# Linear layer's four outer products in one joint tree, and another order of the first loads, in a fused factorization kernel

## The chip, the cores and the metric

The kernel runs on one core of a Trainium2 chip. The time is the device time of one execution in microseconds (us); of several runs the median is given. A profile is one further execution, recorded by the hardware profiler. The engines are TensorE (PE: matmuls, with PEld for its weight loads), VectorE (DVE), ScalarE (ACT), GpSimd (POOL) and SyncE (SP, which here only issues DMAs). Each works through its own list of instructions in order and waits on semaphores for the others.

## The reference

```python
def _L0_rec_ref(x, weight, lin_w, lin_b):   # x 1024x512, weight 64x512x512, lin_w 512x512
    out_lin = x @ lin_w.T + lin_b
    xv = jnp.einsum('bf,efm->bem', x, weight)
    zp = jnp.einsum('bf,efm->bem', jnp.square(x), jnp.square(weight))
    interaction = 0.5 * jnp.sum(jnp.square(xv) - zp, axis=1)
    return out_lin + interaction
```

All is float32. The bulk of the work is `xv`, 64 products of 1024x512 by 512x512. `zp` is summed over the 64 embeddings, so it is one product of squared x with the sum of the squared weights.

## The kernel before

**Products of seven.** Every product of 2x2 blocks is done with seven block products in place of eight (Winograd's form), on two levels. The outer level splits x into A11, A12, A21, A22 (halves of the batch and of the features) and the weight into w11, w12, w21, w22. Outer product i (1 to 7) has its own left operand X_i, a sum of blocks of A, and its own right operand: w11, w21, w22, w21 after an accumulate, T1, T2 or w12 after an accumulate, for i = 1, 2, 3, 4, 5, 6, 7. Here T1 = w11 + w12 and T2 = w11 + w12 + w22. Inside outer product i, `tree` (from line 650) again makes seven block products P1 to P7, each of two 128x512 matmuls. Their right operands are the four blocks of the outer operand and four sums of them, t1 to t4, which GpSimd makes (VectorE makes t1 and t2 of the very first tree). Their left operands are seven slots of the tile `x_all`, four raw blocks and three sums s1, s2, s4, made once at the start by VectorE (`x_sum`, line 413). For the outer operands X5, X7, X6, X3 the four blocks are themselves sums of A's blocks; they are called R5, R7, R6, R3.

**Loops.** The weight comes in 16 groups (`group`, from line 908). A group loads its four quadrants (`load`), forms T1 and T2 (`outer_sum`, line 612), and runs seven trees in the order 1, 6, 2, 7, 5, 4, 3 (1, 2, 6, 7, 5, 4, 3 in the first group). The results are squared by ScalarE, reduced over the embeddings by VectorE (line 339) and collected.

**Inside a tree** the seven products go to PSUM banks in a fixed way: P5 and then P3 to b3, P1 and P2 to b1, P6, P7 and P4 to one of two banks b2. ScalarE copies P5 to a p5 tile, P3 to a p53 tile and P1 into b2, where P6 is added by TensorE. Then results are taken out of the bank after P6 (tile 1), after P2 (tile 0), after P7 (tile 3) and after P4 (tile 2). Since P7 and P4 accumulate in the bank that P6 used, each waits for the add that took the result before. In the first tree these results are the tiles oa0 to oa3: VectorE adds P6's bank to p53 into oa1 and P7's bank to p5 into oa3, both line 316.

**T1 and T2.** In groups 1 to 15 both are made by DMAs: a plain load of w11 and accumulating loads issued by GpSimd (`load_more`, line 604). In group 0 VectorE adds them from the loaded quadrants, T1 in two halves, then T2 in two halves.

**The linear layer** uses the same blocks. Its outer products 1, 2, 4 and 5 are done directly (`lin_product`, line 449) ahead of the first tree; P1 and P2 go in pieces as x and lin_w land. Outer products 6, 7 and 3 are done in one `joint_tree` (line 814), a tree whose seven products run for all members in one go, with 256-column matmuls (line 826). `lin_inner` (line 490) lets GpSimd make the sums of the members' right operands; `lin_tree` (from line 884) adds the members' results up and sends them out by accumulating DMAs. The joint tree is interleaved with the second and third tree of group 0.

**What sets the order.** All operations go through a planner (`Plan`). TensorE's order is fixed by keys: tree number times 7 plus a place from the table `PLACE` (`PLACE_0` in the first tree). The planner lists the other engines' operations by the latest time at which they are due, with costs and landing times written down in the kernel, and emits one list for each engine. The first loads are issued outside it (lines 354 to 386): x and lin_w in pieces on the queues of SP and ACT, each with a written-down landing time.

**Tiles.** x's blocks land in oa0 to oa3 and lin_w's in ob0 and ob1; both sets serve later as results of the trees. `c` (three), `p5` (three), `p53` (three) and `wsq` (two) are rings of tiles.

The lines touched are the tables at the top, the tiles, the first loads, `lin_inner`, `outer_sum`, `tree`, `lin_tree` and `group`.

Of the kernel before, what the change touches and what calls it, by code (L numbers as in the profile page):

```python
# [16 lines left out]
P = 128  # L17
# [8 lines left out]
PLACE = {5: -6, 3: -2, 1: 0, 6: 3, 2: 4, 7: 6, 4: 9}  # L26
PLACE_0 = {**PLACE, 5: -6, 1: -3, 3: -2, 6: -1}
PE, DVE, ACT, POOL, SP = "PE", "DVE", "ACT", "POOL", "SP"
# [3 lines left out]
class Plan:  # L32
# [44 lines left out]
    def order(self):  # L77
# [27 lines left out]
        times = [self.HOP]  # L105
        done, late, nxt, wire = [], 0.0, 0, 9.0

# [95 lines left out]
def kernel(  # L203
# [81 lines left out]
    for q in ("w11", "w12", "w21", "w22a", "w22b", "T1", "T2"):  # L285
        make(q, [P, 2, 2, N])
    for pos in range(4):
        make(f"oa{pos}", half)
        make(f"ob{pos}", half)
    t_ring = {k: ring(f"t{k}", 2, [P, N]) for k in range(1, 5)}  # L290
    p5_ring, p53_ring = ring("p5", 3, half), ring("p53", 3, half)
    c_ring, wsq_ring = ring("c", 3, half), ring("wsq", 2, half)
    make("b1", [P, G, N], ps)
# [61 lines left out]
    def load_x(h, k, lo, hi, at):  # L355

        n, r = f"oa{2 * h + k // KH}", k % KH
        nc.sync.dma_start(buf[n][:, r, lo * Q:hi * Q], x_src[:, k, h * H + lo * Q:h * H + hi * Q])
        for u in range(lo, hi):
            landing((n, r, u), at)  # L360

    def load_lw(queue, ks, c, at):

        l, r = f"ob{ks[0] // KH}", ks[0] % KH
        queue.dma_start(
            buf[l][:, r:r + len(ks), ts(c, N // 2)],
            lw_src[:, ks[0]:ks[0] + len(ks), ts(c, N // 2)],
        )
        for k in ks:
            landing((l, k % KH, c), at)  # L370
# [10 lines left out]
    load_lw(nc.sync, [2, 3], 1, 9.2)  # L381
    for at, k in enumerate((2, 3, 0, 1)):
        load_x(1, k, 0, 2, 10.0 + 0.8 * at)
    nc.scalar.dma_start(bias[:], lin_b)
    landing("bias", 9.5)
# [13 lines left out]

    a_buf = {"A11": "oa0", "A12": "oa1", "A21": "oa2", "A22": "oa3"}  # L400

# [73 lines left out]

    lw_quad = [buf[f"ob{q}"][:, :, ts(c, HM)] for q in range(2) for c in range(2)]
    lw_names = [tuple((f"ob{q}", r, c) for r in range(KH)) for q in range(2) for c in range(2)]
    lt = {
# [11 lines left out]
    def lin_inner():  # L490


        t23 = buf["w22b"].rearrange("p c k n -> p (c k n)")[:, N:3 * N].rearrange(
            "p (i k m) -> p i k m", i=2, k=KH
        )
        flat = buf["ob0"].rearrange("p a (k m) -> p a k m", m=P)
        for (ap, own), t, outs in (
            ((t23, lt_names[2] + lt_names[3]), {k: flat[:, :, k - 1] for k in range(1, 5)}, (6, 7)),
            (rhs[3], {
                k: buf["ob1"][:, (k - 1) // 2, ts((k - 1) % 2, P)] for k in range(1, 5)  # L500
            }, (3,)),
        ):
            b11, b21, b12, b22 = (
                ap[:, k, ts(c, P)] if len(outs) == 1 else ap[:, :, k, ts(c, P)]
                for c in range(2) for k in range(KH)
            )
            names = {k: (("li", outs[0], k),) for k in range(1, 5)}
            more = own + ("quads", "R6")
            for k, x, y, r in (
                (1, b12, b11, more),  # L510
                (2, b22, t[1], more + names[1]),
                (3, b22, b12, more),
                (4, b21, t[2], more + names[2]),
            ):
                costs, emit = two_input(POOL, t[k], x, y, True, len(outs) * P)
                plan.add(costs, emit, r, names[k])
            for at, i in enumerate(outs):
                def of(z):
                    return z[:, at] if len(outs) > 1 else z

                tt[i] = {
                    1: (of(b11), own), 2: (of(b21), own), 3: (of(b22), own),
                    **{p: (of(t[k]), names[k]) for p, k in ((4, 4), (5, 1), (6, 2), (7, 3))},
                }

# [13 lines left out]
    def lin_copy(n, bank, c, sign):  # L539

        for u in range(2):
            plan.add(
                {ACT: 0.56},
                lambda _, u=u: nc.scalar.activation(
                    buf[n][:, u, :], buf[bank][:, u, :], AF.Identity,
                    bias=bias[:, 2 * c + u:2 * c + u + 1], scale=sign,
                ),
                ((bank, u), "bias"), ((n, u),),
            )
        used(n, (n, 0), (n, 1))  # L550
# [6 lines left out]
    def used(*names):  # L557

        plan.add({NONE: 0.0}, None, (), names)

    lin_product(1, "b2_1", True, -1000, by_k=True)
    lin_copy("ob3", "b2_1", 0, 1.0)
    act(buf["ob2"], buf["b2_1"], None, ("b2_1",), ("ob2",))
    lin_product(2, "b1", True, -999, by_k=True)
    lin_last("ob3", "b1", 1)
    lin_store("ob3", 0, 0)
    lin_product(4, "b2_0", True, -998)
    lin_copy("c_2", "b2_0", 0, 1.0)
    lin_store("c_2", 1, 0)
    lin_product(5, "b1", True, -997)  # L570
    flat = buf["w22b"].rearrange("p c k n -> p (c k) n")
    buf["outer7"], buf["negative"] = flat[:, 0::3], flat[:, 1:3]
    used("outer7", ("lt", 1), ("lt", 4))
    lin_copy("outer7", "b1", 1, -1.0)
    lin_store("outer7", 1, 1)
    lin_store("outer7", 0, 1)
    used("quads", *(("ob0", r, c) for r in range(KH) for c in range(2)), ("ob1", 0, 0), ("ob1", 1, 0))
    lin_inner()
# [11 lines left out]

    for n in a_buf.values():
        used(n, *((n, r, u) for r in range(KH) for u in range(2)))


# [5 lines left out]
    def load(g, q):  # L600
        n = w(g, QUAD[q])
        dma(buf[n], weight[g, q], (), (n,), 3.5)

# [8 lines left out]
    def outer_sum(g, which):  # L612
        if g == 0 and which < 3:
            o, a, b = (("T1", "w11", "w12"), ("T2", "w22a", "T1"))[which - 1]
            for c in range(NCB):
                costs, emit = two_input(DVE, buf[o][:, c], buf[a][:, c], buf[b][:, c], False)
                plan.add(costs, emit, (a, b), (o,), both=True)
        elif which < 3:
            n = f"T{which}"
            dma(buf[n], weight[g, 0], (), (n,), 3.5)  # L620
            for q in (1, 3)[:which]:
                load_more(n, weight[g, q])
        elif which == 3:
            load_more("w12", weight[g, 3])
        else:
            load_more("w21", buf["T2"], ("T2",))
# [23 lines left out]
    def tree(s, g, i, order):  # L650
# [3 lines left out]
        for k, a, b, reads in (  # L654
# [6 lines left out]
            costs, emit = two_input(engine, buf[t[k]], a, b, True, 512)  # L661
            plan.add(costs, emit, reads, (t[k],), both=engine == DVE)
        rhs = {
            1: (b11, r), 2: (b21, r), 3: (b22, r), 4: (buf[t[4]], t[4]),
            5: (buf[t[1]], t[1]), 6: (buf[t[2]], t[2]), 7: (buf[t[3]], t[3]),
# [148 lines left out]
    def joint_tree(at, members):  # L814
# [67 lines left out]
        to(2, b2)  # L882

    def lin_tree():

        results = {6: "ob3", 7: "outer7", 3: c_ring()}
        for n in results.values():
            used(n, *((n, pos) for pos in range(4)))
        joint_tree(2, [(i, i, n) for i, n in results.items()])
        for n in results.values():  # L890
            used(n, *((n, pos) for pos in range(4)))
        used("negative", ("lt", 2), ("lt", 3))
        names = tuple(("li", i, k) for i in (6, 3) for k in range(1, 5))
        used("ob0", "quads", *names)
        used("ob1", *lw_names[3], *names)
        o6, o7, o3 = results.values()
        for to, o, a, b, kind in (
            (None, "ob2", "ob2", o6, "a + b"),
            ((0, 1), o3, "ob2", o3, "-a - b"), ((1, 0), o7, "ob2", o7, "a + b"),
        ):  # L900
            x_sum((o,), buf[o], buf[a], buf[b], kind, (a, b), 1024)
            if to:
                lin_add(o, *to)
        act(buf["negative"], buf[o7], "negative", (o7,), ("negative",))
        lin_add("negative", 1, 1)
        used("w22b", "outer7", "negative")

    def group(g, before={}):
        acc_name[g] = acc_ring()
        for q in range(4):  # L910
            load(g, q)
        outer_sum(g, 1)
        outer_sum(g, 2)
        w_squares(g, "w12")
# [31 lines left out]

    def parts(n):
        return tuple((n, pos) for pos in range(4))

    def part(n, pos):  # L950
        q, c = divmod(pos, 2)
        return buf[n][:, c, ts(q, Q)]

    def in_parts(n, *more):
        used(n, *parts(n), *more)

    def halves_of(n):
        for u in range(2):
            buf[n, u] = buf[n][:, u]
            in_parts((n, u), n)  # L960

# [270 lines left out]
```

## Time and profile before

| what | value |
|---|---|
| median of 3 runs | 1402.33 us (1402.14 to 1402.83) |
| the profiled execution | 1403.01 us |
| its span, first to last instruction | 1401.2 us |
| TensorE busy | 1395.3 us |
| VectorE, GpSimd, ScalarE busy | 1099.9, 1053.3, 714.9 us |
| first tree's first matmul | 19.26 us after the start |
| last matmul's start | 1396.93 us |

The span leaves out 1.8 us of the profiled execution's time. In the rows of the profile a matmul in float32 appears as two records, and the next one's start, not its modelled end, tells how long TensorE was held. L316 is the helper's line for every sum of two tiles on VectorE or GpSimd, so a row is told by its tiles: `t<-w` is a sum for a tree, `x_all<-x_all` a sum of x's blocks, `oa<-b,p` a result taken out of a PSUM bank.

### The profile page before, as it was taken

How to read it: one execution, taken by the hardware profiler on the slowest of the kernel's cores; microseconds unless marked ns; L12 is line 12 of the kernel's file. 1: busy time of each engine (PE TensorE's matmuls, PEld its weight loads, DVE VectorE, ACT ScalarE, POOL GpSimd, SP SyncE). 2: the span in 40 equal slices, each digit the busy share in tenths (PEclk: the TensorE clock that was granted, in tenths of full speed). 3: DMA queues.
4: the chain of work that ended last, by engine and by line, in shares of the span. 5: the costliest groups of instructions: out<-in, count | busy, mean ns of one | idle time of the engine just before them, and what ended most of it. 6: DMA issues, size and time to landing. Idle time of an engine off the chain costs nothing.

```text
span 1401.2 us, 10709 instructions
## 1 busy us (share of the span) xinstructions
PE 1395.3 (100%) x3314; PEld 629.8 (45%) x3314; DVE 1099.9 (78%) x987; ACT 714.9 (51%) x756; POOL 1053.3 (75%) x750
## 2 busy tenths in 40 slices
PE   9999999999999999999999999999999999999998
PEld 4544444444444444444444444444444444444454
DVE  7998696877959788696877959678696877959676
ACT  4555473545736456373544636355373544636444
POOL 4796776958778586786958678686786958678994
PEclk9999999999999999999999999999999999999999
DMA  7495574827749285582817538183572817538363
GB/s 270 94 221 162 138 180 121 226 74 180 205 121 232 90 196 164 135 221 82 225 51 180 153 99 206 49 196 120 132 178 84 222 53 180 154 97 207 101 165 113
DMA packets 55815, 212.90 MB, mean 152 GB/s; under 512 B 21520, under 2 KB 23056, under 8 KB 33872
## 3 DMA queue, kind: packets, MB, share of 16 engines
q0 software_dynamic: 13136, 84.81, 31.5%
q1 hardware_dynamic: 40352, 125.12, 25.6%
q10 hardware_dynamic: 2272, 2.30, 0.5%
q8 instruction: 27, 0.44, 0.1%
q14 instruction: 28, 0.23, 0.0%
HBM read 180.75 MB, written 14.02 MB: 139 GB/s over the span
## 4 chain that ended last, share of the span: by engine, by line
PE 96%; DVE 1%; DMA 1%; ACT 0%; issue 0%; SPq 0%; DVEq 0%
PE b L673 93%; PE b L826 2%; PE b L465 1%; DMA c<-xT 1%; PE b L1145 1%; DMA oa<-xT 0%; DVE p L316 0%; DVE c L316 0%; DVE ob L316 0%; DVE w_sum L339 0%; ACT ob L332 0%; DVE oa L316 0%; DVE acc L339 0%; ACT c L332 0%; ACT b L328 0%
## 5 line engine op out<-in xcount | busy, mean ns | idle before, releaser
L673 PE MATMUL b<-t,x_all 128*128 128x512 f32 x1792 | 806.4, 592 | 0.2 <-DVE oa L316 0.2
L673 PEld LDWEIGHTS b<-t,x_all 128*128 128x128 f32 x1792 | 340.2, 190 | 426.1 <-issue 417.3
L673 PE MATMUL b<-w,x_all 128*128 128x512 f32 x768 | 358.1, 592 | 0.0
L316 POOL TENSOR_TENSOR t<-w 128x512 f32<-128x512 f32 x127 | 171.3, 1349 | 148.5 <-PE b L673 78.1
L328 ACT COPY p<-b 128x1024 f32<-128x1024 f32 x165 | 165.6, 1003 | 171.0 <-PE b L673 166.2
L673 PEld LDWEIGHTS b<-w,x_all 128*128 128x128 f32 x768 | 145.9, 190 | 183.7 <-issue 182.5
L316 POOL TENSOR_TENSOR t<-w,t 128x512 f32<-128x512 f32 x127 | 171.8, 1353 | 55.1 <-PE b L673 54.8
L332 ACT ACTIVATE oa<-oa 128x1024 f32<-128x1024 f32 x124 | 129.5, 1057 | 144.2 <-DVE oa L316 144.2
L328 ACT COPY b<-b 128x1024 f32<-128x1024 f32 (+1 forms) x114 | 113.5, 996 | 135.7 <-PE b L673 132.0
L673 PE MATMUL b<-T,x_all 128*128 128x512 f32 x384 | 180.3, 592 | 0.0
L339 DVE TENSOR_REDUCE acc<-oa 128x16 f32<-128x1024 f32 x124 | 148.8, 1211 | 36.7 <-ACT oa L332 36.7
L339 DVE TENSOR_REDUCE w_sum<-wsq 128x16 f32<-128x1024 f32 x128 | 153.6, 1209 | 0.3 <-ACT wsq L332 0.2
L332 ACT ACTIVATE c<-c 128x1024 f32<-128x1024 f32 x77 | 79.6, 1055 | 131.6 <-DVE c L316 88.2
L316 DVE TENSOR_TENSOR oa<-b,p 128x1024 f32<-128x1024 f32 x95 | 115.7, 1218 | 33.7 <-PE b L673 33.5
L316 POOL TENSOR_TENSOR t<-T 128x512 f32<-128x512 f32 x64 | 85.7, 1339 | 53.2 <-issue 31.3
L673 PEld LDWEIGHTS b<-T,x_all 128*128 128x128 f32 x384 | 73.0, 190 | 91.0 <-issue 89.4
L316 DVE TENSOR_TENSOR p<-b,p 128x1024 f32<-128x1024 f32 x79 | 96.4, 1220 | 20.9 <-PE b L673 16.8
L316 DVE TENSOR_TENSOR ob<-b,p 128x1024 f32<-128x1024 f32 x48 | 58.6, 1221 | 64.7 <-PE b L673 64.4
L332 ACT ACTIVATE wsq<-w 128x1024 f32<-128x1024 f32 x96 | 98.3, 1054 | 12.0 <-DMA w<-weight 11.1
L316 POOL TENSOR_TENSOR t<-T,t 128x512 f32<-128x512 f32 x64 | 82.4, 1288 | 20.1 <-PE b L673 20.0
L316 POOL TENSOR_TENSOR c<-oa,p 128x1024 f32<-128x1024 f32 x32 | 84.8, 2651 | 0.0
L316 DVE TENSOR_TENSOR oa<-b,oa 128x1024 f32<-128x1024 f32 x62 | 75.6, 1220 | 9.5 <-PE b L673 9.5
(116 smaller groups left out, 1421.4 us busy)
## 6 DMA issues: line engine op xcount, KB each, us to landing
w<-weight SPq DMA_DIRECT2D x48, 1024.0 KB, 5.4
T<-weight POOLq DMA_DIRECT2D x45, 1024.0 KB, 9.2
T<-weight SPq DMA_DIRECT2D x30, 1024.0 KB, 7.2
w<-weight POOLq DMA_DIRECT2D x16, 1024.0 KB, 11.0
w<-T POOLq DMA_DIRECT2D x16, 1024.0 KB, 6.9
w22a<-weight SPq DMA_DIRECT2D x8, 1024.0 KB, 10.8
w22b<-weight SPq DMA_DIRECT2D x8, 1024.0 KB, 10.9
c<-xT SPq DMA_DIRECT2D x9, 512.0 KB, 6.8
```

The source lines that it names most:

```text
L316: f(o, a, b)
L328: nc.scalar.copy(o, i)
L332: nc.scalar.activation(o, i, func)
L339: lambda _: nc.vector.tensor_reduce(o, i.rearrange("p a (m e) -> p a m e", e=E), axis=AX.X, op=ALU.add),
L465: nc.tensor.matmul(buf[bank][:, c, rows], b[:, k, ts(c, P)], a[:, k, rows], start=first and k == 0 and rows.start == 0, stop=k == KH - 1, ...
L673: nc.tensor.matmul(buf[b][:, j, :], buf[f"X{i}"][:, SLOT[p], ts(j, P)], op, start=first, stop=True, skip_group_check=True,)
L826: nc.tensor.matmul(buf[b][:, u, lo:lo + Q], op[z], buf[f"X{x}"][:, SLOT[p], :], start=first and not lo, stop=True, skip_group_check=True,)
L1145: nc.tensor.matmul(o, ap[:, k, ts(u, P)], in_rows(o, buf[raw[i]][:, k, lo:hi]), start=first and k == 0, stop=k == 1, skip_group_check=True,)
```

## The change

1. **The first tree begins with P1.** `PLACE_0` now orders it 1, 5, 2, 3, 6, then 7 and 4 among the second tree's products. `w11` is loaded in two halves, ahead of two of the eight x pieces.
2. **Linear product 5 joins the tree.** The direct P5 goes. The joint tree has four members, 5, 6, 7, 3; its results go to tiles shared by ob2/ob3 (`ob_all`) and wsq (`wsq01`). `lin_inner` makes four sums of 512 elements in place of eight of 256 and 128, after ScalarE has copied lin_w's block for product 3 beside the others. `lin_tree` adds the results up with five VectorE sums, one accumulating DMA and two plain stores.
3. **Tiles change places.** x lands in ob0 to ob3 and lin_w in oa0 and oa1. The p53 ring has two tiles in place of three, and `lin_p1` holds the first linear product.
4. **T2 of group 0 by DMAs**, as in the other groups: one plain load on SP's queue and two accumulating loads on GpSimd's; w22 is loaded last.
5. The planner's first free time of the DMA wire is 13.5 in place of 9.0.

In the order that comes out, VectorE makes R5, R7, R6 and R3 after the first tree's t1 and t2 (before: R5, R7 and R6 ahead of t1), and the X sums of X4 and X5 stand ahead of the result add of the first tree's P7 (before: after it).

```diff
-PLACE_0 = {**PLACE, 5: -6, 1: -3, 3: -2, 6: -1}
+PLACE_0 = {**PLACE, 1: -6, 5: -5, 2: -4, 3: -3, 6: -2, 7: 3}
...
-        done, late, nxt, wire = [], 0.0, 0, 9.0
+        done, late, nxt, wire = [], 0.0, 0, 13.5
...
+    ob_all = sb.tile([P, 4, 2, N], F32, tag="ob_all", name="ob_all")
...
-    p5_ring, p53_ring = ring("p5", 3, half), ring("p53", 3, half)
-    c_ring, wsq_ring = ring("c", 3, half), ring("wsq", 2, half)
+    p5_ring, p53_ring = ring("p5", 3, half), ring("p53", 2, half)
+    make("lin_p1", half)
+    c_ring = ring("c", 3, half)
+    make("wsq01", [P, 2, 2, N])
...
-    for at, k in enumerate((2, 3, 0, 1)):
+    for at, k in enumerate((2, 3)):
         load_x(1, k, 0, 2, 10.0 + 0.8 * at)
+    for c in range(NCB):
+        nc.sync.dma_start(buf["w11"][:, c], weight[0, 0, :, c])
+        landing(("w11", c), 13.0 + 2 * c)
+    for at, k in enumerate((0, 1)):
+        load_x(1, k, 0, 2, 16.0 + 0.8 * at)
...
+        outs = (5, 6, 7, 3)
+        ap = buf["w22b"].rearrange("p c i (k m) -> p (c i) k m", k=KH)
+        used("t4 used", ("lt", 4))
+        act(ap[:, 3], rhs[3][0], None, rhs[3][1] + ("t4 used",), (("lt", 3, "own"),), 0.56)
...
-    lin_product(5, "b1", True, -997)
...
-        if g == 0 and which < 3:
-            o, a, b = (("T1", "w11", "w12"), ("T2", "w22a", "T1"))[which - 1]
+        if g == 0 and which == 1:
+            o, a, b = "T1", "w11", "w12"
...
-        results = {6: "ob3", 7: "outer7", 3: c_ring()}
+        results = {6: ("ob23", 0), 7: ("ob23", 1), 5: ("wsq01", 0), 3: ("wsq01", 1)}
...
+        for o, a, b in (
+            ("lin_p1", "lin_p1", results[6]), ("sum10", "lin_p1", results[7]),
+            ("sum11", "sum10", results[5]), ("lin_p1", "lin_p1", results[5]),
+            ("lin_p1", "lin_p1", results[3]),
         ):
+            x_sum((o,), buf[o], buf[a], buf[b], "a + b", (a, b), 1024)
+            if o == "sum10":
+                lin_add(o, 1, 0)
+        for n, h in (("sum11", 1), ("lin_p1", 0)):
+            lin_copy(n, n, 1, -1.0)
+            lin_store(n, h, 1)
...
+            load(g, 0)
+            load(g, 2)
+            outer_sum(g, 2)
+            load(g, 1)
+            load(g, 3)
+            outer_sum(g, 1)
```

## The prediction

> **What bounds the kernel now.** I read the page's busy times first, then TensorE's list of waits, then the timelines of TensorE, VectorE and GpSimd over the first 60 us, then the DMA landings there.
>
> ```profile
> span 1401.2 us, 10709 instructions
> ...
> PE 1395.3 (100%) x3314; PEld 629.8 (45%) x3314; DVE 1099.9 (78%) x987; ACT 714.9 (51%) x756; POOL 1053.3 (75%) x750
> ```
> ```profile
> engine line waited for: us in total, times, longest us
> PE b L465 <- DMA oa<-xT: 1.1, 1, 1.1
> PE b L391 <- PEq L1221: 0.8, 1, 0.8
> PE b L673 <- DVE oa L316: 0.2, 1, 0.2
> ```
>
> The second list is all of TensorE's waits in the span. From 7.04 us on TensorE goes without a wait to its last matmul, but for 0.2 us near 461 us. So a change gains only what it takes from TensorE's own work, and it loses whatever makes TensorE wait. Everything is decided where the first tree begins:
>
> ```profile
> 12.30 3.60 PE L465 MATMUL b<-oa,w22b 128*128 128x512 f32 x8
> 15.73 3.60 PE L465 MATMUL b<-x_all,w22b 128*128 128x512 f32 x8
> 19.26 1.98 PE L673 MATMUL b<-t,x_all 128*128 128x512 f32 x4
> ...
> 34.81 1.46 PE L826 MATMUL b<-x_all,ob 128*128 128x256 f32 x6
> 36.10 3.60 PE L673 MATMUL b<-t,x_all 128*128 128x512 f32 x8
> ```
>
> The columns are start, length, engine, line, operation. The row at 15.73 is the direct product P5 of the linear layer (3.43 us to the next row's due start), 19.26 the first tree's first product, 34.81 the joint tree's first product (three members, 1.29 us to the next row), 36.10 the first tree's last product, P4.
>
> **TensorE's work.** Removed: direct P5, 3.43 us. Added: a fourth member in each of the joint tree's seven products, 1.29/3 = 0.43 us each, 3.01 us. Sum: -0.4 us.
>
> **When TensorE wants things now.** With P5 gone the first tree starts at 15.73 instead of 19.16. A product takes 1.72 us, so P5 of it is due at 17.45, P6 at 22.6, P7 at 26.0. P4 stands behind nine tree products and one joint product of four: 15.73 + 10 x 1.72 = 32.9. P4 adds into the bank that held P7, so it waits for VectorE's add of P7 into oa3. Before, P4 came at 36.10 and that add at 33.29: 1.6 us in hand.
>
> **What VectorE has to do first.** In the changed program's order VectorE's operations from the first tree's t1 to that add are: t1, t2, the sums R5, R7, R6, the first sum of X4/X5; then the add of P6 into oa1; then R3 and eight X sums (nine X sums in all; before it was six and half of T1: those of X4/X5 are pulled forward, since member 5 needs X5); then the add into oa3. R5, R7, R6 stood ahead of t1; they come later since w11 is loaded ahead of two x pieces. GpSimd has in the same stretch t3, t4 of tree 1, t1, t3, t2, t4 of tree 2 and the four linear sums, now 512 elements each.
>
> ```profile
> 9.69 0.68 DVE L316 TENSOR_TENSOR w22b<-ob 128x512 f32<-128x512 f32 x1
> ...
> 20.26 1.75 DVE L316 TENSOR_TENSOR t<-w,t 128x512 f32<-128x512 f32 x1
> 21.93 1.76 DVE L316 TENSOR_TENSOR x_all<-x_all 128x512 f32<-128x512 f32 x1
> 23.61 1.76 DVE L316 TENSOR_TENSOR w22b<-ob,ob 128x512 f32<-128x512 f32 x1
> ...
> 33.29 1.23 DVE L316 TENSOR_TENSOR oa<-b,p 128x1024 f32<-128x1024 f32 x1
> ```
> ```profile
> 19.56 3.59 POOL L316 TENSOR_TENSOR t<-w 128x512 f32<-128x512 f32 x2 [0.90 <-DMA w<-weight]
> 23.10 3.41 POOL L316 TENSOR_TENSOR t<-w,t 128x512 f32<-128x512 f32 x2
> 26.47 0.91 POOL L316 TENSOR_TENSOR ob<-w22b 128x256 f32<-128x256 f32 x1
> ...
> 39.02 1.26 POOL L316 TENSOR_TENSOR t<-T 128x512 f32<-128x512 f32 x1 [1.73 <-DVE T L316]
> ```
>
> The reader is to see turns being taken: alone a 512-element sum is 0.6 us on VectorE (9.69 to the next start, 10.29) and 1.26 on GpSimd; side by side each takes 1.7, one operation of each per 1.69 us ((26.47 - 23.10)/2). So one GpSimd operation goes in between any two VectorE sums that read SBUF, and costs VectorE 1.69 - 0.60 = 1.08 us; alone it is 1.23 from start to start. I take 1.15. The adds that read PSUM (1.14) take no part in the turns: the one at 27.85 has its usual 1.21. By the same rows 1024-element sums cost VectorE 1.13 (14.04 to 16.31 for two), 256-element ones 0.33.
>
> **The walk.** w11's second half: w11 landed at 17.02 (9.59 + 7.4, below), and moves ahead of two x pieces that landed 0.63 apart, so 17.02 - 1.25 = 15.8; bounds 15.1 (a w11 at the later loads' 2.5 us per MB) and 17.0.
>
> ```profile
> w<-weight SPq DMA_DIRECT2D x1, 1024.0 KB, 7.4
> ```
>
> First part, from 15.85: t1, t2 0.6 each, three of 1.13, one of 0.6, in all 5.2; four GpSimd turns 4.6: 25.65. Add of P6 (P6 itself is long done): 26.8. P7, due 26.0, waits for this: **0.8 us**. Second part: 1.13 + five of 0.6 + three of 0.33 = 5.1; five GpSimd turns (its sixth hides behind the add) 5.75: 37.65. Add of P7 1.14: 38.8. P4 starts at 38.9 instead of 32.9: **6.0 us** in all, P7's 0.8 included. Queued behind P4 on TensorE is everything else, so it goes into the end in full. With turns at 1.08 and 1.23 it is 5.4 and 6.7; with the landing's bounds 5.3 and 7.2.
>
> **T2 by DMAs.** Two VectorE additions and their wait go (they ended at 38.8); added are one 1 MB load on SP's queue and two accumulating loads on GpSimd's. The rows have such loads at 7.0, 8.1 and 10.5 us from issue to landing. The second is issued behind the four linear sums, near 36, and lands at 44 to 46.5. Behind it on GpSimd stand the w12 accumulate, which waits for T1's second half on VectorE (38.8 + 1.13 + two reductions of 1.12 + 1.13, 43.3; 1.0 to issue), and a 2.33 add that waits for VectorE until 45.6, then T2's first sum: 45.6 + 2.33 + 1.23 = 49.2, plus 0.1. The third tree's P5 wants it six products after P4, at 49.2: **0.1 us**. The DMAs are hidden by the lateness above; without that cover they cost up to 3.9 (second rival).
>
> **The clock.** At the end the granted clock falls some 3 us after the last matmul (1397.3); at the start four matmul records take 2.9 us where the size needs 1.3, so 1.6 is lost:
>
> ```profile
> 0.78 2.90 PE L391 MATMUL b<-const-float32-0.0 128*128 128x512 f32 x4 [0.78 <-PEq L1221]
> ```
> ```profile
> 1397.40:1400.00 2.60, 0.00 (x0) 0.00 (x0) 0.65 (x2) 0.00 (x0) 0.00 (x0) 1.00 0.88 314
> 1400.00:1401.20 1.20, 0.00 (x0) 0.00 (x0) 0.00 (x0) 0.00 (x0) 0.00 (x0) 0.64 0.00 0
> ```
>
> (The clock is the last column but two.) The wait before P4, 5.2 us without a matmul, is longer than that 3 us, so a drop is likely. Between 0 and 1.6 I take **1.2**, nearer the upper row.
>
> The Trainium skill ("TensorE: Matmul & The Clock Gate", Part 1: The HAM clock gate) says that a free-running window of 3.4 us without work halves the clock and that a busy window restores it. By the page a drop costs up to half of a window, an estimate of 1.7, and a gap of 5.2 us holds a whole window only in about half of the phases, so the sum could be 1.2 lower in some runs; the rows agree as far as they go.
>
> **The rest at nothing.** Linear stores and sums lie beside TensorE; SP's first stores and w22a move behind the new T2 load (w22a, no longer summed into T2, is next read near 70 us). The p53 ring of two instead of three: its copies come back two trees (24 us) later; were the cover gone, one 2.4 us GpSimd add. Squares buffers lent to the linear results: ScalarE is busy 51%. Past the joint tree TensorE's order is the same. Between 0 and 1.2 (one VectorE operation late); I take 0, since past 60 us TensorE waits for 0.2 us in all.
>
> **Sum.** -0.4 + 6.0 + 0.1 + 1.2 = +6.9. The profiled execution took 1403.01 (span 1401.2, 1.8 around it) and would take 1409.9; the median of the runs, 0.7 lower, becomes **1409.2**.
>
> **Rivals.**
> 1. *Not slower: GpSimd doesn't get its turns in the second part.* VectorE then does R3 and the eight X sums back to back: 26.8 + 5.1 + 1.14 = 33.1, and P4, already moved by P7's 0.8, finds the add done. Lost 0.8, net +0.4: 1402.7. Each operation let in adds 1.15; lost time passes 3.2 (net 0.2%) from the third of five on. Against it: in 21.9 to 26.5 every VectorE sum has one GpSimd operation ahead of it. For it: GpSimd's linear sums wait for R3 and might start late. 11%.
> 2. *T2's DMAs are what is late.* Without most of the turns P4 is on time and the third tree's P5 is due at 43.2; T2 lands between 41 (two loads of 8.1 from 24.9) and 46 (two of 10.5), its first sum 1.2 later: 0 to 3.9 late, 2.0 in the middle: 1403.9. For it: 10.5 is seen with other transfers about, as here. 10%.
> 3. *w11 is not earlier* (17.0) and the turns cost 1.23: the same wait at 7.9, the clock 1.6: 1411.5. 12%, and 4% beyond 1412.5.
>
> **The numbers.** Forecast (1406 to 1411) 63%, rivals 11, 10, 12 and 4. The range 1403 to 1412.5 takes in all but the first rival and what lies beyond, 15 in 100. A measurement of this kernel can tell about 0.2% (2.8 us) from no change. Within that: rival 1 and half of rival 2, 15%; faster by more has no mechanism, since TensorE's work falls by 0.4 alone: 1%; slower 84%.
>
> **What will show it.** TensorE's waits should have an entry of the tree's matmuls on VectorE's oa add, some 5 us once and near 0.8 once, at 33 to 39 us; VectorE's X sums there should be 1.2 to 1.8 long beside GpSimd's t and ob sums; the granted clock should dip once near 39 us. X sums at 0.4 to 0.7 and an add of P7 before 33 would make it wrong; so would a wait on GpSimd's t from T2.

## The result, and the profile after

| | before | changed | ratio, 95% interval |
|---|---|---|---|
| the result: median | 1402.71 us | 1409.86 us (5 runs: 1409.42, 1409.64, 1409.86, 1411.18, 1416.94) | 1.0062, 1.0051 to 1.0073 |
| the same kernel again | 1402.63 us | 1410.26 us (5 runs, 1409.37 to 1410.71) | 1.0053, 1.0040 to 1.0066 |

The ratio compares the means of the runs, without one run of before that took 5594.90 us; the long execution is in it, and the ratio of the medians in the first row is 1.0051.

By the medians the change costs 7.2 to 7.6 us; the forecast was 1409.2, which is 6.9 above before. The profile that came with the result is that of its longest execution, 1416.94 us (span 1415.2). I took a second one of the same kernel, 1409.37 us (span 1407.6); I call them the long and the short execution. TensorE's list of waits in the long one (columns: us in total, times, longest):

```profile
PE b L677 <- DVE oa L328: 5.2, 2, 5.0
PE b L830 <- DVE wsq L869: 4.5, 1, 4.5
```

and in the short one:

```profile
PE b L677 <- DVE oa L328: 5.0, 1, 5.0
```

The entry that both have is the forecast one: the tree's matmul (L677) waits for VectorE's add into oa (L328 is the sum helper, L316 before). The other, a joint-tree matmul (L830) that waits 4.5 us, was not foreseen. In TensorE's timeline of the long execution the first stands here (start, length, engine, line, operation):

```profile
38.23 6.61 PE L677 MATMUL b<-t,x_all 128*128 128x512 f32 x8 [5.03 <-DVE oa L328]
```

This is the first tree's P4 and what follows it; the other wait ends at 64.84. Its eight records take 6.61 us; before, such a row of eight took 3.60. The clock was at half, as the busy times of one and the same stretch show, in the long execution and then in the short one (the granted clock is the last column but two):

```profile
37.28:44.12 6.84, 5.89 (x7) 2.52 (x8) 6.54 (x6) 3.13 (x4) 0.86 (x1) 0.50 0.66 134
```
```profile
37.28:44.12 6.84, 5.88 (x10) 2.65 (x11) 6.84 (x7) 3.28 (x4) 0.86 (x1) 0.75 0.68 134
```

In the long execution the clock is at half for the whole stretch of 6.84 us, in the short one for half of it. In what follows the time lost at a matmul is its start minus the start of the one before, minus the usual step (0.43 us for 512 columns, 0.22 for 256). So counted, TensorE loses this from 10 us on:

| place | forecast | short | long |
|---|---|---|---|
| P7 of the first tree, 26 us | 0.8 | 0.26 | 0.36 |
| P4 of the first tree, 38 us | 5.2 | 5.20 | 5.20 |
| half clock behind P4 | 1.2 | 1.72 | 2.98 |
| third tree, for T2 | 0.1 | 0 | 0 |
| joint tree, 65 us, and half clock behind it | none | 0 | 4.68 + 1.65 |

For the short execution: 7.18 in all, less 0.42 of TensorE's work, less 0.36 and 0.19 that before lost near 461 and 19 us, less 0.23 by which the first tree begins earlier than 15.73, is 5.98; the last matmul ends 5.99 later than in before (1403.30 and 1397.31). What comes behind the last matmul is another 0.4 longer (4.26 us for 3.89), which makes the 6.4 between the two profiled executions.

**Where the 8 us of the long execution come from.** Its VectorE timeline has one sum of x's blocks that takes 8.26 us, and GpSimd's has this at the time:

```profile
54.99 8.26 DVE L328 TENSOR_TENSOR x_all<-x_all 128x512 f32<-128x512 f32 x1
```
```profile
52.17 0.85 POOL L611 DMA_DIRECT2D w<-T  x1
52.90 1.43 POOL L328 TENSOR_TENSOR t<-w 128x512 f32<-128x512 f32 x1
54.12 1.42 POOL L328 TENSOR_TENSOR t<-T 128x512 f32<-128x512 f32 x1
...
59.03 2.45 POOL L328 TENSOR_TENSOR c<-c,oa 128x1024 f32<-128x1024 f32 x1
```

In the short execution the same instructions:

```profile
53.83 1.69 DVE L328 TENSOR_TENSOR x_all<-x_all 128x512 f32<-128x512 f32 x1
```
```profile
51.05 0.85 POOL L611 DMA_DIRECT2D w<-T  x1
53.72 1.26 POOL L328 TENSOR_TENSOR t<-w 128x512 f32<-128x512 f32 x1 [1.82 <-DMA w<-weight]
```

Behind P4 the long execution lost 1.26 us more to the clock; GpSimd, which gets its work from TensorE by way of VectorE's adds, is 1.1 later there (52.17 against 51.05), and the load that `t<-w` needs landed 0.8 earlier (52.81 against 53.64). So there GpSimd's sums follow close on the issue of a DMA (the first starts within the issue's 0.85 us), and VectorE's sum gets in only when six of them are done, the one that ran when it came and five more; in the short execution GpSimd waits 1.82 us for the load, and VectorE has its usual turn. From two executions this is only argued; the second half of the experiments tests it.

### The profile page after: what moved, and what is told of

The parts are those of the page before. It is cut to its first block, busy times and chain, and to the rows that moved or that the text cites. A ratio compares the mean times of both kernels' runs of the same rounds, so it can differ in the third digit from the quotient of the medians.

```text
span 1415.2 us, 10730 instructions
## 1 busy us (share of the span) xinstructions
PE 1400.4 (99%) x3320; PEld 634.0 (45%) x3320; DVE 1110.0 (78%) x985; ACT 718.3 (51%) x756; POOL 1051.8 (74%) x746
## 4 chain that ended last, share of the span: by engine, by line
PE 96%; DVE 2%; DMA 1%; issue 1%; ACTq 0%; SPq 0%; DVEq 0%
PE b L677 94%; PE b L830 1%; DVE x_all L328 1%; PE b L1163 1%; DMA w<-weight 0%; DMA oa<-lin_wT 0%; DVE x_all L438 0%; DVE w_sum L351 0%; DVE oa L328 0%; DVE t L328 0%; DVE c L328 0%; DVE p L328 0%; ACTq L377 0%; DVE T L1142 0%; DVE wsq L869 0%
## 5 line engine op out<-in xcount | busy, mean ns | idle before, releaser
L677 PE MATMUL b<-t,x_all 128*128 128x512 f32 x1792 | 809.5, 594 | 5.2 <-DVE oa L328 5.2
L677 PEld LDWEIGHTS b<-t,x_all 128*128 128x128 f32 x1792 | 341.3, 191 | 432.9 <-issue 418.5
L677 PE MATMUL b<-w,x_all 128*128 128x512 f32 x768 | 358.1, 592 | 0.0
L328 POOL TENSOR_TENSOR t<-w 128x512 f32<-128x512 f32 x127 | 170.3, 1341 | 155.4 <-PE b L677 88.0
L677 PEld LDWEIGHTS b<-w,x_all 128*128 128x128 f32 x768 | 145.9, 190 | 183.8 <-issue 182.6
L328 POOL TENSOR_TENSOR t<-w,t 128x512 f32<-128x512 f32 x127 | 169.9, 1337 | 56.3 <-PE b L677 54.7
L340 ACT COPY b<-b 128x1024 f32<-128x1024 f32 x114 | 113.7, 997 | 135.5 <-PE b L677 132.4
L677 PE MATMUL b<-T,x_all 128*128 128x512 f32 x384 | 180.4, 592 | 0.0
L328 DVE TENSOR_TENSOR oa<-b,p 128x1024 f32<-128x1024 f32 x95 | 115.6, 1217 | 36.4 <-PE b L677 36.1
L328 POOL TENSOR_TENSOR t<-T 128x512 f32<-128x512 f32 x64 | 84.4, 1319 | 53.9 <-issue 31.0
L677 PEld LDWEIGHTS b<-T,x_all 128*128 128x128 f32 x384 | 73.0, 190 | 91.1 <-issue 87.8
L328 DVE TENSOR_TENSOR p<-b,p 128x1024 f32<-128x1024 f32 x79 | 96.4, 1220 | 20.9 <-PE b L677 16.8
L328 DVE TENSOR_TENSOR ob_all<-b,p 128x1024 f32<-128x1024 f32 x48 | 58.6, 1221 | 64.8 <-PE b L677 64.8
L328 POOL TENSOR_TENSOR t<-T,t 128x512 f32<-128x512 f32 x64 | 82.8, 1294 | 19.2 <-PE b L677 19.1
L328 POOL TENSOR_TENSOR c<-oa,p 128x1024 f32<-128x1024 f32 x32 | 84.9, 2654 | 0.0
L328 DVE TENSOR_TENSOR oa<-b,oa 128x1024 f32<-128x1024 f32 x62 | 75.6, 1219 | 9.6 <-PE b L677 9.6
```

Of the source, the lines that this page charges most:

```text
L328: f(o, a, b)
L340: nc.scalar.copy(o, i)
L677: nc.tensor.matmul(buf[b][:, j, :], buf[f"X{i}"][:, SLOT[p], ts(j, P)], op, start=first, stop=True, skip_group_check=True,)
```

## The experiments

The theory: VectorE's and GpSimd's turns delay the add of P7, TensorE waits for it, and the wait halves the clock. The first rival: the DMAs for T2 cost the time. A second question came with the long execution: what makes a sum of VectorE take 8 us.

**`again`: the changed kernel, unedited.**

> The changed kernel once more, unedited, to have its time on the chip of this group of runs and a second profile. Theory (turns of VectorE and GpSimd hold up the first tree, and the wait slows the clock): TensorE waits for VectorE's oa add for 5.2 us at 38 us and 0.3 to 0.8 us at 26 us, the granted clock falls to 0.5 for two windows of 3.4 us behind it, about 1409.6 us. Second theory (the 8.26 us sum of VectorE seen once at 55 us belongs to every execution): it is in this profile too, with a wait of some 4.5 us of the joint tree. If it is an accident of one execution, no VectorE sum is over 3 us here and TensorE's time is some 6 us below that profile.

Measured: 1410.26 (ratio 1.0053, 1.0040 to 1.0066), P4's wait 5.0 in the list, P7's loss 0.26; no instruction of VectorE over 2.3 us. The 8.26 us sum is an accident of some executions. The clock was at half for one stretch of 3.4 us, not two.

**`copies`: fewer turns.** In `lin_inner`:

```diff
-            costs, emit = two_input(POOL, t[k], x, y, True, len(outs) * P)
-            plan.add(costs, emit, r, names[k])
+            act(t[k], x, None, r, names[k], 0.56)
```

> The four sums of the linear layer's inner trees are ScalarE copies of their first operand instead of GpSimd sums, so this arithmetic is left out and the linear outputs aren't the reference's; all else is as in the changed kernel. Theory (turns): with four GpSimd operations fewer in VectorE's way, the add of P7 ends near 33.9 instead of 38.2, P4's wait is 1.1 instead of 5.2, there is no clock drop near 39, waits of 0.4 to 1.0 come up at 44 and 54; 3.2 us of waits and 3.0 us of clock less than the changed kernel: about 1403.4. Rival (T2's accumulating DMAs, or their issue by GpSimd, are what holds up the start): P4's wait stays at about 5 and the time within 1 us of the changed kernel's.

Measured: 1406.16 (1.0023, 1.0014 to 1.0032), 4.1 below `again`. P4 loses 0.92 in place of 5.20, P7 0.40, and the clock stays at 1.0. With the four operations gone most of the wait goes, and the drop with it, so the theory holds and the rival falls. The expected time was too low by 2.8. It took 3.0 for a clock drop that costs 1.72 in `again`, and the waits fell by 2.0 in place of 3.2, since two others came up: 0.53 at 17.8, where TensorE waits for the first tree's t, and 1.63 at 55.5, where the joint tree waits for VectorE (0.4 to 1.0 at 44 and 54 was expected). The rest is the base, 1410.26 in this group for the 1409.6 assumed.

**`warm`: TensorE kept at work in the wait.** Ahead of P4, in `tree`:

```diff
+        if at == 2:
+            def idle(_):
+                for j in range(5):
+                    nc.tensor.matmul(buf["b3"][:, 0, :], zero[:, 0:P], zero, start=False, stop=True,
+                                     skip_group_check=True)
+            plan.add({PE: 0.05}, idle, ("b3",), ("b3",), key=8.5)
```

> Five matmuls by zeros (512 columns, 0.43 us each) stand ahead of the first tree's P4, adding nothing to their bank; the wait for VectorE is cut into pieces under 3.4 us. Theory (the clock has a price of its own): 2.15 us of work added, about 2.9 us of waits gone by a walk of the instructions' order, which moves a little, and the clock stays at 1.0 near 39 us, 3.0 us gained: 1405.9, some 3.7 below the changed kernel. Rival (the wait alone costs, the clock's fall is paid for by work that would wait anyway): some 0.7 below, 1408.9.

Measured: 1409.25 (1.0049, 1.0035 to 1.0063). The filler was twice as long as I had counted: five float32 matmuls are ten records, 4.3 us. So neither number stands as written, though the time is near the rival's, but the profile can be read. P4 starts at 38.25 (38.24 in `again`), so the filler lies in the wait and delays nothing, and the clock stays at 1.0. Of the 1.72 that the drop cost in `again`, 0.94 comes back as two waits for VectorE's sums at 45.6 and 47.9, which the slower clock had hidden, and the last matmul ends 0.6 earlier. The median is 1.0 lower, but the two sets of runs overlap (1408.76 to 1410.37 and 1409.37 to 1410.71). By these two profiles the drop costs less than the time it takes from the matmuls.

**`t2vec`: T2 of group 0 by VectorE, as before.**

```diff
-        if g == 0 and which == 1:
-            o, a, b = "T1", "w11", "w12"
+        if g == 0 and which < 3:
+            o, a, b = (("T1", "w11", "w12"), ("T2", "w22a", "T1"))[which - 1]
...
+        for q in range(4):
+            load(g, q)
+        outer_sum(g, 1)
+        outer_sum(g, 2)
```

> T2 of group 0 is made by VectorE again, with the loads in the order of before; all else is as in the changed kernel. Theory (turns): the two additions come behind the wait, so P4's wait stays at 5.0, and the additions come back as waits of the third tree and behind it (1.3 at 49.5, 0.7 in all later): about 1.4 above the changed kernel, 1411. Rival (T2's DMAs are what costs): the time falls towards that of before, below 1406.

Measured: 1418.50 (1.0112, 1.0098 to 1.0126). P4's wait stays (4.5), as the theory says, but the time is 7 us above its number. In the profile a 256-column sum of VectorE takes 6.79 us at 56.81, behind a DMA issue of GpSimd at 53.98 and under four of its sums, and the joint tree waits 5.5 us. That looks like the long execution's trouble again; all four runs lie at 1417.6 to 1419.0, one of them is profiled.

**`late`: three of the linear sums behind the add of P7.**

```diff
-            plan.add(costs, emit, r, names[k])
+            if k in (2, 3, 4):
+                lin_late.append((costs, emit, r + ('oa3',), names[k]))
+            else:
+                plan.add(costs, emit, r, names[k])
...
+        for late in lin_late:
+            plan.add(*late)
```

> Three of GpSimd's four sums for the linear inner trees are ordered behind the first tree's add of P7, nothing is left out. Theory (turns): VectorE has three turns fewer to give ahead of that add, P4's wait falls from 5.2 to 3.0 or 3.3, and the time by 2.3 from the waits and by up to 1.7 from a clock that drops later or not at all: 1406 to 1408. Rival (VectorE is late from its own work, and GpSimd's operations only use its gaps): P4's wait and the time stay as in the changed kernel, 1410.

Measured: 1407.55, 1407.66, 1407.98, and 1417.67, 1418.46, 1419.36, 1419.95 (median 1417.67, ratio 1.0079, 1.0051 to 1.0106). The three are where the theory puts them, with P4's loss at 3.05. The four are 10 us above. The profile is of one of the three: its longest sum of VectorE takes 2.96 us, and the clock stays at 1.0. What the four did differently no profile shows.

**`filled`: P4 behind more products as well.** The edit of `late`, and

```diff
-PLACE_0 = {**PLACE, 1: -6, 5: -5, 2: -4, 3: -3, 6: -2, 7: 3}
+PLACE_0 = {**PLACE, 1: -6, 5: -5, 2: -4, 3: -3, 6: -2, 7: 3, 4: 11.5}
...
-                        cost += 0.9 * over
-                        longer(POOL, 0.35 * over)
+                        cost += 1.0 * over
...
-                        cost += 0.5 * over
-                        longer(DVE, 0.9 * over)
+                        cost += 1.0 * over
```

> As the run before, and P4 of the first tree goes behind more products of the second tree, with the planner told that VectorE's and GpSimd's sums take strict turns; nothing is left out. Theory (what costs is VectorE being late at one place, and the clock behind it): no wait over 1 us is left ahead of 60 us, the clock stays at 1.0, 4.6 us of waits and 1.7 to 3.0 of clock less than the changed kernel: 1403.5, within 0.2 per cent of the kernel before. Rival (the start as a whole has too much to do for VectorE, so that a wait filled is a wait moved): waits of 3 to 5 us come up at 44 to 60, 1408 to 1410.

Measured: 1410.07 (1.0046, 1.0033 to 1.0059): the rival's number, and its waits (2.1 at 42.3, 1.0 at 47.4, 2.3 at 58.4). But the profile has two long sums of VectorE, 5.32 us at 34.69 and 3.89 at 52.62, each behind a DMA issue of GpSimd. So the run couldn't decide until those were dealt with; `filled_paced` below does.

**`oldload`: the order of loads and of products of before.** The table `PLACE_0` is that of before, and the four x pieces stand ahead of w11:

```diff
-PLACE_0 = {**PLACE, 1: -6, 5: -5, 2: -4, 3: -3, 6: -2, 7: 3}
+PLACE_0 = {**PLACE, 5: -6, 1: -3, 3: -2, 6: -1}
...
-    for at, k in enumerate((2, 3)):
+    for at, k in enumerate((2, 3, 0, 1)):
```

> P1 first and w11 ahead of two x pieces are both undone, with the order of products and of loads of before; joint tree of four, tiles and T2 by DMAs as in the changed kernel. Theory (VectorE's and GpSimd's sums ahead of the add of P7 set the start, wherever TensorE begins): TensorE waits 4.6 us ahead of its first tree and 0.6 at P4 instead of 5.2 at P4, the clock drops at 19 us instead of 39: 1409 to 1411. Rival (the early start of the first tree is what puts it in front of VectorE's sums, and costs): the time falls by over 3 us, to 1406.5 or less.

Measured: 1414.37 (1.0080, 1.0068 to 1.0092). TensorE waits 5.7 ahead of the first tree and 3.2 at P4, and the clock falls twice. The rival's 1406.5 didn't come, but the theory's 1409 to 1411 and its wait of 0.6 at P4 didn't either: a sum of VectorE took 8.71 us at 29.40, behind a DMA issue at 29.14 and under six sums of GpSimd. What the early start of the first tree is worth by itself stays open.

**`turns`: the long sums by themselves.** Each trial, with GpSimd's six sums back to back and VectorE's sum behind two fillers of varied length:

```python
nc.vector.tensor_add(a[:, 0:512], bank[:, 0:512], d[:, 0:512])     # both engines start here
if issue:
    nc.vector.tensor_add(src, bank[:, 0:512], d[:, 0:512])
    nc.gpsimd.dma_start(dst, src, accum_op=ALU.add)
for k in range(6):
    nc.gpsimd.tensor_sub(g[k], a[:, 0:512], a[:, 512:1024])
...
nc.vector.tensor_sub(probe[:, 0:512], x[:, 0:512], y[:, 0:512])
```

> A kernel of trials by itself, which leaves out the whole computation: GpSimd gets six two-input sums of 512 columns back to back, VectorE a two-input sum of 512 columns from SBUF, which comes in 33 ns steps at another point of a GpSimd sum (42 trials); then 28 trials with an accumulating DMA issued by GpSimd ahead of its sums. First theory (phase): the sum has its turn after the GpSimd sum that runs, 1.7 us or less, but where it comes some 0.55 to 0.6 us ahead of that one's end (as in the two sums of 8.26 and 6.79 us) it is passed over by all that follow, 4 to 6 us, with and without the DMA. Second theory (DMA): it is passed over only where GpSimd has just issued a DMA. Third (neither): no sum is over 2 us in any trial, and what does it stays open.

Measured: in the 42 trials without a DMA VectorE's sum takes 0.69 to 1.79 us, whatever the point at which it comes. In the 28 with one it takes 5.6 to 7.1 us: in every one it is passed over by all of GpSimd's sums that are left. The first theory falls, the second stands. One trial of each kind, VectorE and GpSimd (in the first, GpSimd's first sum lies ahead of the rows, from 277.23):

```profile
278.45 6.59 POOL L53 TENSOR_TENSOR g<-a 128x512 f32<-128x512 f32 x5
279.04 1.22 DVE L58 TENSOR_TENSOR probe<-x,y 128x512 f32<-128x512 f32 x1
```
```profile
372.90 1.01 POOL L51 DMA_DIRECT2D dst<-src  x1 [1.64 <-DVE src L50]
373.64 7.63 POOL L53 TENSOR_TENSOR g<-a 128x512 f32<-128x512 f32 x6
...
374.69 7.14 DVE L58 TENSOR_TENSOR probe<-x,y 128x512 f32<-128x512 f32 x1
```

The probe at 374.69 ends when GpSimd's sixth sum has ended. A mark to look for: in that state GpSimd's sums are recorded with some 1.55 us each, in the others with 1.26, though they follow each other at 1.22 in both. In the long execution above they are recorded with 1.36 to 1.43.

**`turns2`: what starts and what ends it.** The same trial with one thing changed at a time:

```python
nc.gpsimd.dma_start(dst, src)                                      # plain
nc.gpsimd.memset(small[:, 0:64], 0.0)                              # or a copy, or a sum of 64 columns
for k, n in enumerate(acts):                                       # the first sum waits for ScalarE
    nc.scalar.copy(late[:, 0:n], d[:, 0:n] if k else src[:, 0:n])
```

> Trials by themselves again, the computation left out. In the trials before, VectorE's sum was passed over by all of GpSimd's sums in each of the 28 with a DMA issued by GpSimd ahead and in none of the 42 without. Now GpSimd gets, ahead of its sums: nothing; an accumulating DMA; a plain DMA; the accumulating DMA and then a small copy, a memset or a sum of 64 columns; twelve or three sums instead of six; or the first sum also waits for ScalarE, which ends at steps before and behind the end of the issue. First theory (the state lasts until GpSimd is idle once, whatever moves): sums directly behind an issue pass VectorE's, with a plain DMA too and through all twelve; a wait of some tenths of a us behind the issue ends it, and VectorE's sum takes 1.8 us or less. Second (the DMA in flight or its first 2 to 3 us are what does it): with twelve sums VectorE gets its turn midway, and a wait under 2 us changes nothing. The small operations between tell which of them ends it: unknown, both ends are 1.8 and 6 us.

| behind GpSimd's DMA issue | VectorE's sum, us |
|---|---|
| no DMA (4 trials) | 0.73 to 1.62 |
| accumulating DMA, six sums (4) | 5.72 to 6.88 |
| plain DMA, six sums (4) | 5.46 to 6.45 |
| a copy, a memset or a 64-column sum, then six sums (12) | 5.80 to 6.98 |
| three sums (1), twelve sums (1) | 2.41, 13.65 |
| first sum needs ScalarE, which is done before the issue ends (2) | 5.71, 6.38 |
| first sum waits for ScalarE and starts 0.02 to 1.87 us after the issue's end (22) | 0.69 to 1.74 |

The trial of twelve:

```profile
252.02 0.87 POOL L57 DMA_DIRECT2D dst<-src  x1 [2.06 <-DVE src L50]
252.63 14.91 POOL L66 TENSOR_TENSOR g<-a 128x512 f32<-128x512 f32 x12
...
254.44 13.65 DVE L71 TENSOR_TENSOR probe<-x,y 128x512 f32<-128x512 f32 x1
```

This DMA has landed at 255.34, and VectorE's sum goes on waiting until GpSimd's twelfth sum has ended at 267.54: it isn't the transfer that it waits for. The first theory holds, with one word changed: the state begins with a GpSimd sum directly behind a DMA issue and lasts as long as GpSimd has sums to go on with, and it doesn't come up if the first sum really has to wait. The length of the gap says nothing: with the plain DMA the first sum starts 0.02 us behind the issue and the state is there, with ScalarE done 0.13 us before the issue's end it starts 0.02 us behind it too and the state is not. With ScalarE done 0.5 us before the end, so that GpSimd has nothing to wait for, it is there. With the plain DMA the sums are recorded with 1.26 us, so the mark above may be missing.

How long GpSimd has to wait isn't settled. The shortest wait of the trials that kept the state away moved the first sum from 0.61 to 0.89 us behind the issue's start. In the kernel's long execution the first sum seems to have waited as well: it starts 0.73 us behind the issue's start and 0.09 behind the landing of its load at 52.81. This wait, some 0.1 us and over before the issue's end, did not keep the state away.

**Back in the kernel: `late_paced`, `filled_paced`, `t2vec_paced`.** Each is the kernel of that name with one pause behind each of GpSimd's first five DMA issues (in `load_more`), and the same order of all else:

```diff
+            nc.gpsimd.dma_start(view(buf[n]), src, accum_op=ALU.add)
+            if paused:
+                nc.gpsimd.memset(pause[0], 0.0)
+                nc.scalar.copy(pause[1], pause[0])
+                nc.gpsimd.tensor_copy(pause[2], pause[1])
```

> The kernel with three linear sums later, in the same order on every engine, but behind each of GpSimd's first five DMA issues GpSimd waits once for ScalarE (a memset of one column, ScalarE's copy of it, GpSimd's copy of that); nothing is left out. Its executions without the pause lay at 1407.6 to 1408.0 and at 1417.7 to 1420. Theory (a GpSimd sum directly behind a DMA issue lets no sum of VectorE in until GpSimd waits): no execution is in the upper group, the pauses themselves cost 0.4 by a walk of the order: 1408.0, all within 1.5. Rival (the upper group has another cause, the clock for one): both groups stay, a median of 1418 or a spread of 10.

> The same pauses in the kernel with P4 behind more products and three linear sums later, whose profile had two sums of VectorE of 5.3 and 3.9 us behind DMA issues; nothing is left out. Theory: no sum of VectorE is over 2.5 us, the waits of TensorE after 30 us fall from 6.4 to some 2.4, none over 1 us, and the clock stays at 1.0: 1405.5 to 1406. Rival (the waits come from VectorE's order, not from these sums): within 1 of 1410.

> The same pauses in the kernel with T2 of group 0 by VectorE, which lay at 1418.5 with one sum of VectorE of 6.8 us behind a DMA issue; nothing is left out. Theory: that sum is under 2.5 us, the wait of the joint tree behind it (5.5) goes, and what is left is the price of the two additions: 1.4 above the changed kernel and 0.6 for the pauses, 1412. Rival (T2's additions by VectorE cost 8 by themselves): 1418.

| | without the pauses | with them | ratio with, 95% interval |
|---|---|---|---|
| late | 1407.6 to 1408.0, and 1417.7 to 1420.0 | 1408.39 (1408.36 to 1409.97) | 1.0046, 1.0033 to 1.0059 |
| filled | 1410.07 | 1405.09 (1404.67 to 1406.06) | 1.0018, 1.0009 to 1.0026 |
| t2vec | 1418.50 | 1410.75 (1409.91 to 1411.64) | 1.0059, 1.0045 to 1.0073 |

All three go the theory's way; no sum of VectorE over 2.8 us is left in any of their profiles. Some details were missed: `late_paced` spreads over 1.6 us in place of 1.5, and its P4 loses 3.56 with a clock drop of one window, where the profile of `late` has 3.05 and none; `filled_paced` has one sum of 2.71 us and one wait of 1.1, for GpSimd's t at 44.3, and its median is 0.4 under the range expected. That the upper group of `late` was made of passed-over sums is argued from its absence in the five runs with the pauses. The second sum of T1 (`T<-w,w`) in `filled`, and the same instruction in `filled_paced`, with what GpSimd does beside it in the latter:

```profile
34.69 5.32 DVE L326 TENSOR_TENSOR T<-w,w 128x1024 f32<-128x1024 f32 x1
```
```profile
34.72 1.21 DVE L326 TENSOR_TENSOR T<-w,w 128x1024 f32<-128x1024 f32 x1
```
```profile
34.20 0.88 POOL L617 DMA_DIRECT2D T<-weight  x1 [3.56 <-DMA T<-weight]
34.78 0.41 POOL L619 MEMSET pause<- 128x1 f32 x1
35.48 0.49 POOL L621 COPY pause<-pause 128x1 f32<-128x1 f32 x1 [0.29 <-ACT pause L620]
```

GpSimd waits 0.29 us for ScalarE, its next sum starts 1.0 later than without the pause (35.93 for 34.91), and VectorE gets 4.1 back. Here VectorE's sum is over when GpSimd's next one starts, so the pause may only have left it room. In `t2vec` and `t2vec_paced` it can be seen to get its turn again, between two sums of GpSimd:

```profile
56.81 6.79 DVE L328 TENSOR_TENSOR x_all<-x_all 128x256 f32<-128x256 f32 x1
```
```profile
57.46 1.37 DVE L328 TENSOR_TENSOR x_all<-x_all 128x256 f32<-128x256 f32 x1
```
```profile
57.29 1.26 POOL L328 TENSOR_TENSOR t<-T,t 128x512 f32<-128x512 f32 x1
58.52 1.45 POOL L328 TENSOR_TENSOR t<-w,t 128x512 f32<-128x512 f32 x1
```

`filled_paced` is the best version found: 5 us below the changed kernel and 2.4 above before. `t2vec_paced` is within 0.5 of the changed kernel, where 2 were expected. So T2's additions by VectorE cost next to nothing, and the 8 us of `t2vec` were the passed-over sum and what followed from it. The changed kernel with the pauses alone was not run.

## Why the prediction was right, point by point

The mechanism came as forecast, a wait of P4 for VectorE's add of P7 that goes when GpSimd's sums are taken away. That the sum is within 0.7 us of the median is in part luck: in the short execution P7's term was 0.5 too large and the clock's 0.5 too small. The terms that the sum lacked (a first tree 0.2 earlier, 0.55 that before itself loses, an end 0.4 longer) come to -0.4: from one profiled execution to the other 6.9 was forecast and 6.4 came.

- **TensorE's work, -0.4.** As said: a product of the joint tree is now eight records of 256 columns and takes 1.73 us (46.39 to 48.12 in the long execution), for six in 1.29.
- **The turns.** Right in kind and size. VectorE's eight X sums ahead of the add of P7 run from 27.58 to 37.04, each recorded with 1.48 to 1.77 us while GpSimd has sums, then with 0.68 and 0.41. The two parts of the walk: the second took 10.97 us from the end of one add to the start of the next (26.00 to 36.97), for 10.85 in the walk. `copies` and `late` take turns away and P4's wait falls by 4.3 and 2.2.
- **w11's second half, 15.8.** Too late: it landed at 15.03, just ahead of my lower bound of 15.1. So the add of P6 ended at 26.00, not 26.8, and P7 lost 0.26 to 0.36, not 0.8.
- **P4, 5.2.** 5.20, though the add ended at 38.17 and not 38.8: TensorE came to P4 as much earlier, since the first tree began at 15.40 and 15.50 (15.73 in the sum) and P7's wait was shorter. The match to the hundredth is luck.
- **T2, 0.1.** No wait at the third tree's P5. T2 landed at 43.0, a little before the 44 to 46.5 counted. The second rival (its DMAs late) didn't come.
- **The clock, 1.2 (0 to 1.6).** The mechanism was right, the term too small: 1.72 in the short execution, 2.98 in the long one. The bound of 1.6 came from the start of the kernel, where only that part of the slow stretch counts that lies behind the first matmul (from 0.78 to about 4.3 us in before). The Trainium skill ("TensorE: Matmul & The Clock Gate", Part 1) gives free-running windows of 3413 ns; here the half clock lasts from 37.285 to 44.112, 6.83 us, in the long execution and half of that in the short one. A wait of 5.2 may thus cost one window or two; which of them the eight executions without a profile had isn't known. Part of this price comes back as waits when the clock stays up (0.94 of 1.72 in `warm`).
- **The rest at nothing, 0 to 1.2.** This is where the prediction failed to see: between 50 and 65 us a VectorE sum can be passed over by GpSimd's, and take 8 us. Past 60 us I had argued from TensorE's 0.2 us of waits in the profile of before, which can't tell what a shift of 1 us does. The median hides it, one of ten executions shows it.

## What to carry to other kernels

In these runs a GpSimd sum directly behind a DMA that GpSimd issues shut out VectorE's sums of two SBUF tiles until GpSimd had to wait for something: look there for VectorE instructions several times their usual length, and put one real wait behind the issue (here 1 us of GpSimd for 4.1 and 5.4 us of VectorE). Time taken from TensorE just ahead of a place where two other engines share turns can come back as waiting: here the 3.4 us of the direct product came back as 5.5 us of waits and 1.7 us of slow matmuls. Three sums later, the pauses, and the waiting product behind others that are ready regained 5 us together; without the last of these (and its planner costs), in `late_paced`, the time is 3.3 higher. A kernel that has runs 10 us apart deserves a look at which instruction differs, before its median is compared.

## What the runs showed of the hardware that was not expected

- Turns: in 42 trials at 33 ns steps VectorE's two-input sum got in behind the GpSimd sum that ran (0.69 to 1.79 us). The Trainium skill ("SBUF — State Buffer", SBUF: two separate sides) tells of an exclusive lock held for one whole instruction; those trials agree. Behind a DMA issue they don't: the lock, if it is one, lasted through twelve instructions (13.65 us). Why an issue has this effect, and why a pause ends it, the runs don't show.
- In the changed kernel's long execution an earlier issue, at 24.26, did no harm: there the second sum reads what the first has just written, and it starts 1.65 us after that one's start, where sums back to back follow at 1.22. That fits a pause that ends the state; it was not tried by itself.
- Five float32 matmuls of 512 columns by a constant are ten records of 0.43 us.
